# Two attentions of a four-layer fp32 kernel: transposed output, tokens as weights, and tanh read from PSUM

## The chip, the cores and the metric

The kernel runs on one core of a Trainium2 chip. One launch computes a whole network of four layers. The metric is device time in microseconds (us). Before the change it is 10574.42 us, the median of 3 runs (10572.73 to 10580.19).

Engines are named as in the profile: PE is the matrix engine's matmul and PEld its weight load, DVE the vector engine, ACT the scalar engine, POOL GpSimd, SP the engine that issues transfers. Everything is fp32.

## The reference, cut to what matters

The input is 4 images of 56 x 56 tokens with 128 channels, so S = 3136 tokens an image. Layers 0 and 1 (a windowed attention and a selective scan) and the two feed-forward parts are not touched by the change. The two attentions that are:

```python
def _L2_attn_ref(x, W1, b1, w2, b2):             # x: layer norm of t
    f = jnp.einsum('bih,ha->bia', x, W1[:h])     # a: 16 hidden units
    g = jnp.einsum('bjh,ha->bja', x, W1[h:])
    t = jnp.tanh(f[:, :, None, :] + g[:, None, :, :] + b1)
    scores = jnp.einsum('bija,a->bij', t, w2[:, 0]) + b2[0]
    flag = jnp.tril(jnp.ones((n_seq, n_seq)), -1)     # key j before query i only
    e = jnp.exp(scores) * flag
    w = e / (jnp.sum(e, axis=-1, keepdims=True) + 1e-10)
    return jnp.einsum('bij,bjh->bih', w, x)

def _L3_attn_ref(x):                             # x: layer norm of t
    scores = jnp.einsum('bsd,btd->bst', x, x)
    return jnp.einsum('bst,btd->bsd', jax.nn.softmax(scores, axis=-1), x)

def _ln_t(v, eps=1e-5):                          # normal over channels: they sum to zero
    m = jnp.mean(v, axis=-1, keepdims=True)
    return (v - m) / jnp.sqrt(jnp.var(v, axis=-1, keepdims=True) + eps)
...
t = t + _L2_attn_ref(_ln_t(t), ...)
t = t + _L2_ffn_ref(_ln_t(t), ...)
t = t + _L3_attn_ref(_ln_t(t))
t = t + _L3_ffn_ref(_ln_t(t), ...)
```

Layer 2 takes a tanh for every pair of tokens and every one of 16 hidden units, for the lower triangle only. Layer 3 is a plain softmax attention of x with itself over the full square, and subtracts a constant (64) in place of the row maximum.

## The kernel before

The kernel is written in a tile framework that sets semaphores, gives out buffers of a pool (`bufs` of them for a tag) and orders each engine's instructions itself: an instruction that is ready early may be placed ahead of its place in the program. Tokens are cut into 28 tiles of TP = 112, and into 7 chunks of CH = 448 queries (TC = 4 tiles). `xT` is the normed image with channels on the partitions, `xa` the same with tokens on the partitions and a column of ones, so that the product with the weights `e` gives the sum of them in column 128.

```python
def normed(self, b, big, sm, psum, tag):
    xa = self.t(big, [TP, NT, C + 1], "xa")
    self.nc.gpsimd.memset(xa[:, :, C : C + 1], 1.0)
    self.layer_norm(b, sm, xa)
    xT = self.t(big, [P, S], "xT")
    for c in range(NCH):
        self.transposed_chunk(psum, tag, xa, c, xT[:, c * CH : (c + 1) * CH])   # 4 transposes, one copy on DVE or ACT in turn
    return xa, xT
```

Layer 2. One tanh instruction takes 8 keys x 16 hidden units on the 128 partitions and 448 queries in the free dimension; its bias is `g`, one value a partition. A key tile of 112 tokens needs NG = 14 of them. A matmul with 32 columns of weights (`place`) sums the hidden units and puts the 8 rows where they belong.

```python
for b in range(B):
    xa, xT = self.normed(b, big, sm, ps_m, "m")
    fT = self.t(big, [P, S], "fT")
    for c in range(NCH):                       # line 821: 7 matmuls and 7 copies an image
        ps = self.t(ps_m, [P, 512], "m")
        nc.tensor.matmul(ps[:, :CH], wf..., xT[:, c * CH : (c + 1) * CH], start=True, stop=True)
        nc.vector.tensor_copy(fT[:, c * CH : (c + 1) * CH], ps[:, :CH])
    ps = self.t(ps_m, [P, 512], "m")
    for j in range(JG): ...                    # line 828: 8 matmuls for g
    g = ...
    for c in range(NCH):
        self.additive_chunk(b, c, xa, fT, g, b2, place, later, sm, ps_s, ps_o)

def additive_chunk(self, b, c, xa, fT, g, b2, place, later, sm, ps_s, ps_o):
    po = [self.t(ps_o, [P, 512], f"o{s}") for s in range(TC)]      # four banks
    for J in range(TC * (c + 1)):              # key tiles up to the diagonal
        k = max(J - TC * c, 0)
        lo = k * TP
        ps = self.t(ps_s, [P, 512], "s")
        for q in range(TC):
            for blk in range(4):
                n = 4 * blk + q
                if n >= NG: continue
                th = self.t(sm, [P, CH], "th", bufs=8)
                at = NG * J + n
                nc.scalar.activation(          # line 852
                    th[:, lo:], fT[:, c * CH + lo : (c + 1) * CH], AF.Tanh, bias=g[:, at : at + 1])
                ...
                nc.tensor.matmul(              # line 857
                    ps[QW * blk : QW * blk + rows, lo:CH], place[:, off : off + rows], th[:, lo:], ...)
        e = self.t(sm, [TP, CH], "e", bufs=3)
        nc.scalar.activation(e[:, lo:], ps[:TP, lo:CH], AF.Exp, bias=b2)       # line 862
        if J >= TC * c:
            nc.gpsimd.tensor_mul(e[:, lo : lo + TP], e[:, lo : lo + TP], later)
        for s in range(k, TC):                 # line 866: e is the weight, 129 columns stream
            nc.tensor.matmul(
                po[s][:TP, : C + 1], e[:, s * TP : (s + 1) * TP], xa[:, J, :],
                start=(J == 0), stop=(J == TC * c + s))
    self.attended(b, c, po, 1e-10, sm)

def attended(self, b, c, po, eps, sm):
    for s in range(TC):
        den = self.t(sm, [TP, 1], "den", bufs=4)
        nc.vector.tensor_scalar(den, po[s][:TP, C : C + 1], eps, None, op0=ALU.add)
        nc.vector.reciprocal(den, den)
        x = self.X[b][:, TC * c + s, :]
        nc.vector.scalar_tensor_tensor(x, po[s][:TP, :C], den, x, op0=ALU.mult, op1=ALU.add)
```

Layer 3, the attention of one image:

```python
xa, xT = self.normed(b, big, sm, ps_s, "s")
for c in range(NCH):
    po = [self.t(ps_o, [P, 512], f"o{s}") for s in range(TC)]
    for t in range(NT):                        # 28 key tiles of 112
        ps = self.t(ps_s, [P, 512], "s")
        nc.tensor.matmul(                      # line 1050
            ps[:TP, :CH], xT[:, t * TP : (t + 1) * TP], xT[:, c * CH : (c + 1) * CH], start=True, stop=True)
        e = self.t(sm, [TP, CH], "e", bufs=3)
        nc.scalar.activation(e, ps[:TP, :CH], AF.Exp, bias=shift)              # line 1055
        for s in range(TC):                    # line 1057
            nc.tensor.matmul(
                po[s][:TP, : C + 1], e[:, s * TP : (s + 1) * TP], xa[:, t, :],
                start=(t == 0), stop=(t == NT - 1))
    self.attended(b, c, po, 0.0, sm)
```

Of the kernel before, what the change touches and what calls it, by code (L numbers as in the profile page):

```python
# [10 lines left out]
AF = mybir.ActivationFunctionType  # L11
# [45 lines left out]
def host_constants():  # L57
# [11 lines left out]
    p = np.arange(P)  # L69
    place = np.zeros((P, QW + QW - JG), np.float32)  # L70
# [4 lines left out]
    for q in range(QG):  # L75
        pick[:, q, :] = (p % HD // 8 == q)[:, None] & (p[None, :] // DS == p[:, None] % 8)
        back[p, q, 8 * q + p // DS] = 1.0
    return {
        "k_state": (p[None, :] % DS == np.arange(DS)[:, None]).astype(np.float32),
# [9 lines left out]
class Hybrid:  # L89
# [688 lines left out]

    def normed(self, b, big, sm, psum, tag):

        xa = self.t(big, [TP, NT, C + 1], "xa")
        self.nc.gpsimd.memset(xa[:, :, C : C + 1], 1.0)  # L782
        self.layer_norm(b, sm, xa)
        xT = self.t(big, [P, S], "xT")
        for c in range(NCH):
            self.transposed_chunk(psum, tag, xa, c, xT[:, c * CH : (c + 1) * CH])
        return xa, xT

    def layer2_attention(self):
        nc, a, tc = self.nc, self.a, self.tc  # L790
        with ExitStack() as ctx:
# [17 lines left out]
            later = self.load(wp, [TP, TP], "later", a["k_later"])  # L809

            big = ctx.enter_context(tc.tile_pool(name="l2_big", bufs=2))
            sm = ctx.enter_context(tc.tile_pool(name="l2_sm", bufs=2))
            ps_m = ctx.enter_context(tc.tile_pool(name="l2_m", bufs=2, space=PSUM))
            ps_s = ctx.enter_context(tc.tile_pool(name="l2_s", bufs=2, space=PSUM))
            ps_o = ctx.enter_context(tc.tile_pool(name="l2_o", bufs=1, space=PSUM))
            for b in range(B):
                xa, xT = self.normed(b, big, sm, ps_m, "m")
                fT = self.t(big, [P, S], "fT")
                for c in range(NCH):
                    ps = self.t(ps_m, [P, 512], "m")  # L820
                    nc.tensor.matmul(
                        ps[:, :CH], wf.rearrange("p j a -> p (j a)"), xT[:, c * CH : (c + 1) * CH],
                        start=True, stop=True,
                    )
                    nc.vector.tensor_copy(fT[:, c * CH : (c + 1) * CH], ps[:, :CH])
# [8 lines left out]
                for c in range(NCH):  # L834
                    self.additive_chunk(b, c, xa, fT, g, b2, place, later, sm, ps_s, ps_o)

    def additive_chunk(self, b, c, xa, fT, g, b2, place, later, sm, ps_s, ps_o):
        nc = self.nc
        po = [self.t(ps_o, [P, 512], f"o{s}") for s in range(TC)]
        for J in range(TC * (c + 1)):  # L840
            k = max(J - TC * c, 0)
            lo = k * TP
            ps = self.t(ps_s, [P, 512], "s")

            for q in range(TC):
                for blk in range(4):
                    n = 4 * blk + q
                    if n >= NG:
                        continue
                    th = self.t(sm, [P, CH], "th", bufs=8)  # L850
                    at = NG * J + n
                    nc.scalar.activation(  # L852
                        th[:, lo:], fT[:, c * CH + lo : (c + 1) * CH], AF.Tanh, bias=g[:, at : at + 1]
                    )
# [10 lines left out]
            for s in range(k, TC):  # L865
                nc.tensor.matmul(  # L866
                    po[s][:TP, : C + 1], e[:, s * TP : (s + 1) * TP], xa[:, J, :],
                    start=(J == 0), stop=(J == TC * c + s),
                )
        self.attended(b, c, po, 1e-10, sm)  # L870

    def attended(self, b, c, po, eps, sm):

        nc = self.nc
        for s in range(TC):
            den = self.t(sm, [TP, 1], "den", bufs=4)
            nc.vector.tensor_scalar(den, po[s][:TP, C : C + 1], eps, None, op0=ALU.add)  # L877
            nc.vector.reciprocal(den, den)
            x = self.X[b][:, TC * c + s, :]
            nc.vector.scalar_tensor_tensor(x, po[s][:TP, :C], den, x, op0=ALU.mult, op1=ALU.add)  # L880
# [147 lines left out]
    def layer3(self, attention=True, ffn=True):  # L1028
        nc, a, tc = self.nc, self.a, self.tc
        with ExitStack() as ctx:  # L1030
# [5 lines left out]
            shift = self.t(wp, [TP, 1], "shift")  # L1036
            nc.vector.memset(shift, SHIFT3)

            big = ctx.enter_context(tc.tile_pool(name="l3_big", bufs=2))
            sm = ctx.enter_context(tc.tile_pool(name="l3_sm", bufs=2))  # L1040
            ps_s = ctx.enter_context(tc.tile_pool(name="l3_s", bufs=4, space=PSUM))
            ps_o = ctx.enter_context(tc.tile_pool(name="l3_o", bufs=1, space=PSUM))
# [136 lines left out]
```

## Time and profile before

The profiled execution took 10590.0 us. The stages, with the busy time of the engines in each, from the profile's view by stretches of time:

| stage | from, to (us) | length | PE | ACT | DVE | granted PE clock |
|---|---|---|---|---|---|---|
| layer 0 | 0 to 1050 | 1050 | 860.93 | 255.03 | 452.68 | 0.82 |
| layer 1 | 1050 to 4371 | 3321 | 2972.43 | 1712.61 | 2982.67 | 0.89 |
| layer 2, attention, 4 images | 4371 to 8191 | 3820 | see below | see below | 127.78 | 1.00 |
| layer 2, feed-forward | 8191 to 8694 | 503 | 404.83 | 49.86 | 148.72 | 0.51 |
| layer 3, attention of image 0 | 8694 to 9045 | 351 | see below | see below | 20.18 | 0.99 |
| layer 3, feed-forward of image 0 | 9045 to 9170 | 125 | 92.57 | 8.70 | 103.25 | 0.80 |

The last two rows come again for images 1 to 3. The four attentions of layer 3, from the first matmul of line 1050 to the end of the last of line 1057, take 350.2, 348.9, 347.9 and 348.5 us.

How to read it: a row of instruction groups names line, engine, operation, the tile written and the tile read, their shapes, the count, busy time, the mean of one in ns, and the idle time of that engine just before, with what ended it. An fp32 matmul is two records in the trace, each with a weight load of its own: the 784 x 4 matmuls of line 1057 are 6272 records. A row of the timeline has start, length, engine, line, operation and how many like instructions were merged. The length of a merged row runs from the first start to the last end, and neighbours overlap.

### The profile page before, as it was taken

The page shows a single profiled execution, that of the slowest core. Times are in us where ns is not written, and L with a number is a line of the kernel's source. Part 1 is how long each engine was busy: PE and PEld are TensorE (multiplying, and loading weights), DVE is VectorE, ACT ScalarE, POOL GpSimd, SP SyncE. Part 2 cuts the span into 40 slices and gives each one's busy share as a digit, 9 for nine tenths or more (in the row PEclk, how much of TensorE's full clock was granted, in tenths as well). Part 3 has the DMA queues.
Part 4 walks back from the last instruction along what each step waited for, and adds up shares of the span by engine and source line. Part 5 has one row for each costly group of instructions (what it writes and reads, how often), then busy time and mean ns, then how long its engine had stood idle before and what let it go on. Part 6 is the DMA issues. An engine that isn't in the chain of part 4 may idle for free.

```text
span 10590.0 us, 117304 instructions
## 1 busy us (share of the span) xinstructions
PE 9694.1 (92%) x45951; PEld 4085.7 (39%) x45951; DVE 4189.2 (40%) x8326; ACT 6116.9 (58%) x10038; POOL 2520.1 (24%) x1478
## 2 busy tenths in 40 slices
PE   7888799999899999899999999999999799898998
PEld 3333233333333333333333333333332586565665
DVE  3444798999998989500000000000000310413223
ACT  2222455555555555599989989998998103232222
POOL 0000577777777777200000000000000000000000
PEclk8788888998999889899999999999999559999999
DMA  2000000000000000000000000000000120000000
GB/s 40 1 1 6 5 1 1 1 1 1 1 1 1 1 1 1 1 1 1 1 1 1 1 1 1 1 1 1 1 1 15 39 78 1 7 1 7 1 7 7
DMA packets 90718, 61.20 MB, mean 6 GB/s; under 512 B 20635, under 2 KB 81587, under 8 KB 89971
## 3 DMA queue, kind: packets, MB, share of 16 engines
q1 hardware_dynamic: 90165, 53.70, 1.9%
q8 instruction: 362, 5.93, 0.2%
q14 instruction: 191, 1.56, 0.1%
HBM read 46.61 MB, written 7.07 MB: 5 GB/s over the span
## 4 chain that ended last, share of the span: by engine, by line
PE 74%; DVE 11%; ACT 9%; issue 4%; POOL 1%; SPq 0%; DMA 0%; ACTq 0%; DVEq 0%; POOLq 0%
PE s L857 27%; PE o L1057 7%; PE s L1050 6%; DVE hs L573 5%; PE a L551 5%; PE o L866 4%; PE m L680 4%; ACT e L862 2%; PE y L583 2%; PE d L407 2%; PE o L407 2%; PE s L390 2%; PE s L1127 1%; PE u L558 1%; DVE dBu L568 1%
## 5 line engine op out<-in xcount | busy, mean ns | idle before, releaser
L852 ACT ACTIVATE th<-fT,g 128x448 f32<-128x448 f32 (+3 forms) x6272 | 3328.9, 622 | 17.5 <-DVE g L833 17.5
L857 PE MATMUL s<-th,place 128*32 128x448 f32 (+4 forms) x12544 | 3182.7, 516 | 7.0 <-ACT th L852 7.0
L577 POOL TENSOR_TENSOR hs<-hs,bc 128x896 f32<-128x896 f32 x896 | 1857.8, 2082 | 701.0 <-DVE hs L573 588.2
L877 DVE TENSOR_SCALAR den<-o 112x1 f32<-112x1 f32 x224 | 31.8, 152 | 4961.7 <-PE o L866 3642.8
L573 DVE TENSOR_TENSOR_SCAN hs<-a,dBu 128x448 f32<-128x448 f32 x1792 | 1847.7, 1072 | 161.7 <-POOL hs L577 86.1
L857 PEld LDWEIGHTS s<-th,place 128*32 128x32 f32 (+1 forms) x12544 | 787.0, 106 | 2131.0 <-ACT th L852 2031.5
L561 ACT ACTIVATE a<-a 128x896 f32<-128x896 f32 x896 | 808.5, 902 | 953.2 <-PE u L558 442.3
L551 PE MATMUL a<-delta,A_pick 32*128 32x448 f32 x3584 | 1079.8, 638 | 96.7 <-DVE hs L573 92.4
L558 PE MATMUL u<-du,pick 32*128 32x448 f32 x3584 | 1034.7, 657 | 32.1 <-DVE dBu L568 27.8
L568 DVE TENSOR_TENSOR dBu<-u,bc 128x448 f32<-128x448 f32 x1792 | 1016.9, 609 | 46.5 <-PE u L558 41.3
L1055 ACT ACTIVATE e<-s,shift 112x448 f32<-112x448 f32 x784 | 496.3, 634 | 887.7 <-PE s L1050 840.3
L864 POOL TENSOR_TENSOR e<-e,later 112x112 f32<-112x112 f32 x112 | 47.2, 422 | 3814.4 <-ACT e L862 3814.4
L1057 PEld LDWEIGHTS o<-xa,e 112*112 112x112 f32 x6272 | 711.1, 176 | 297.5 <-ACT e L1055 295.6
L1057 PE MATMUL o<-xa,e 112*112 112x129 f32 x6272 | 789.3, 279 | 13.5 <-ACT e L1055 0.9
L1050 PE MATMUL s<-xT 128*112 128x448 f32 x1568 | 655.9, 540 | 0.0
L551 PEld LDWEIGHTS a<-delta,A_pick 32*128 32x128 f32 x3584 | 338.4, 202 | 707.5 <-issue 326.4
L866 PE MATMUL o<-xa,e 112*112 112x129 f32 x3248 | 492.3, 288 | 105.5 <-ACT e L862 98.1
L866 PEld LDWEIGHTS o<-xa,e 112*112 112x112 f32 x3248 | 384.5, 176 | 446.3 <-ACT e L862 402.2
L395 ACT ACTIVATE e<-s 112x896 f32<-112x896 f32 (+1 forms) x272 | 206.4, 801 | 601.8 <-PE s L390 434.7
L583 PE MATMUL y<-hs,sum 128*32 128x448 f32 x3584 | 495.7, 628 | 3.6 <-POOL hs L577 3.6
L782 POOL MEMSET xa<- 112x28 f32 x12 | 1.6, 148 | 1822.0 <-DVE X L880 1280.2
L558 PEld LDWEIGHTS u<-du,pick 32*128 32x128 f32 x3584 | 300.2, 204 | 302.9 <-DVE dBu L568 300.1
(225 smaller groups left out, 8436.3 us busy)
## 6 DMA issues: line engine op xcount, KB each, us to landing
w<-in_L_ffn_weight SPq DMA_DIRECT2D x16, 1024.0 KB
w<-in_L_ffn_weight SPq DMA_DIRECT2D x64, 256.0 KB
X<-in_x SPq DMA_DIRECT2D x8, 784.0 KB
out<-X SPq DMA_DIRECT2D x8, 784.0 KB
e_edge<-dtab SPq DMA_DIRECT2D x42, 49.0 KB
cw<-in_L_conv_conv_w SPq DMA_DIRECT2D x1, 1024.0 KB
e_inner<-dtab SPq DMA_DIRECT2D x14, 49.0 KB
dtab<-tab SPq DMA_DIRECT2D x1, 637.0 KB
```

What stands on the lines that cost most here:

```text
L551: nc.tensor.matmul(A[p][:, k], w["A"][own, l, f, q, :], pre[j]["delta"][own, f], start=True, stop=True,)
L558: nc.tensor.matmul(U[p][:, k], w["pick"][own, q, :], pre[j]["du"][own, f], start=True, stop=True)
L561: nc.scalar.activation(A[p], A[p], AF.Exp)
L568: nc.vector.tensor_mul(V[p][:, k], u[:, k], pre[p // PAIRS]["bc"][:, 0])
L573: nc.vector.tensor_tensor_scan(HS[p][:, k], A[p][:, k], V[p][:, k], 0.0, op0=ALU.mult, op1=ALU.add)
L577: nc.gpsimd.tensor_mul(HS[p], HS[p], bc[:, 1:2].to_broadcast([P, 2, CH]))
L583: nc.tensor.matmul(py[j, f][r * HD : (r + 1) * HD, :], w["sum"][:, q, :], HS[p + r // 2][:, r % 2], start=False, stop=(q == QG - 1),)
L852: nc.scalar.activation(th[:, lo:], fT[:, c * CH + lo : (c + 1) * CH], AF.Tanh, bias=g[:, at : at + 1])
L857: nc.tensor.matmul(ps[QW * blk : QW * blk + rows, lo:CH], place[:, off : off + rows], th[:, lo:], start=(q == 0), stop=(n + 1 == NG or q = ...
L866: nc.tensor.matmul(po[s][:TP, : C + 1], e[:, s * TP : (s + 1) * TP], xa[:, J, :], start=(J == 0), stop=(J == TC * c + s),)
L1050: nc.tensor.matmul(ps[:TP, :CH], xT[:, t * TP : (t + 1) * TP], xT[:, c * CH : (c + 1) * CH], start=True, stop=True,)
L1057: nc.tensor.matmul(po[s][:TP, : C + 1], e[:, s * TP : (s + 1) * TP], xa[:, t, :], start=(t == 0), stop=(t == NT - 1),)
```

## The change

The product of weights and values is turned around in both attentions. Before, the weights `e` were the array's stationary operand, in four pieces of 112 queries, and 129 columns of values streamed through. Afterwards the values (`xa[:, J, :]`, tokens on the partitions) are stationary and all 448 queries stream in one matmul; the result `po` has channels on the partitions and lies in one bank. No column is left over for the ones, so they take the place of channel 127, and `attended` turns the result back with a constant matrix `back`: an identity whose column 127 is -1 in every other row (the normed channels sum to zero) and whose column 128 picks the sum of the weights.

Besides, in layer 2 the first term `f` is no longer copied to SBUF: it is computed a chunk at a time into its own pool of two PSUM banks, and tanh reads it there. Its buffers `th` go from 8 to 12. In layer 3 the keys are cut into 25 tiles (24 of 128 and one of 64) in place of 28 of 112, for which the values are transposed again from `xT` into `xk`, and the program puts the product of a tile two tiles after its scores.

```diff
+    back_out = np.eye(P, P + 1, dtype=np.float32)
+    back_out[:, P - 1] = -1.0
+    back_out[P - 1, P - 1] = 0.0
+    back_out[P - 1, P] = 1.0
...
-        xa = self.t(big, [TP, NT, C + 1], "xa")
-        self.nc.gpsimd.memset(xa[:, :, C : C + 1], 1.0)
+        xa = self.t(big, [TP, NT, C], "xa")
... layer 2
+            ps_f = ctx.enter_context(tc.tile_pool(name="l2_f", bufs=2, space=PSUM))
-            ps_o = ctx.enter_context(tc.tile_pool(name="l2_o", bufs=1, space=PSUM))
+            ps_o = ctx.enter_context(tc.tile_pool(name="l2_o", bufs=2, space=PSUM))
             for b in range(B):
                 xa, xT = self.normed(b, big, sm, ps_m, "m")
-                fT = self.t(big, [P, S], "fT")
-                for c in range(NCH):
-                    ... (7 matmuls into ps_m, 7 copies to fT)
+                nc.gpsimd.memset(xa[:, :, C - 1 : C], 1.0)
...
                 for c in range(NCH):
-                    self.additive_chunk(b, c, xa, fT, g, b2, place, later, sm, ps_s, ps_o)
+                    f = self.t(ps_f, [P, 512], "f")[:, :CH]
+                    nc.tensor.matmul(f, wf..., xT[:, c * CH : (c + 1) * CH], start=True, stop=True)
+                    po = self.additive_chunk(c, xa, f, g, b2, place, later, sm, ps_s, ps_o)
+                    self.attended(b, c, po, 1e-10, back, sm, ps_m, "m")
... additive_chunk
-        po = [self.t(ps_o, [P, 512], f"o{s}") for s in range(TC)]
+        po = self.t(ps_o, [P, 512], "o")[:, :CH]
-                    th = self.t(sm, [P, CH], "th", bufs=8)
+                    th = self.t(sm, [P, CH], "th", bufs=12)
-                    nc.scalar.activation(
-                        th[:, lo:], fT[:, c * CH + lo : (c + 1) * CH], AF.Tanh, bias=g[:, at : at + 1]
-                    )
+                    nc.scalar.activation(th[:, lo:], f[:, lo:], AF.Tanh, bias=g[:, at : at + 1])
-            for s in range(k, TC):
-                nc.tensor.matmul(po[s][:TP, : C + 1], e[:, s * TP : (s + 1) * TP], xa[:, J, :], ...)
+            nc.tensor.matmul(po[:, lo:], xa[:, J, :], e[:, lo:], start=(J == 0), stop=(J == last))
... attended
+        oT = self.t(sm, [P, CH], "oT")
+        nc.vector.tensor_copy(oT, po)
+        for s in range(0, TC, 2):
+            ps = self.t(psum, [P, 512], tag)[:TP, : 2 * (C + 1)].rearrange("p (k c) -> p k c", k=2)
+            for k in range(2):
+                nc.tensor.matmul(
+                    ps[:, k, :], oT[:, (s + k) * TP : (s + k + 1) * TP], back, start=True, stop=True)
+            den = ... (as before, two tiles at a time; reads ps)
... layer 3
+                    tiles = [(k, min(P, S - k)) for k in range(0, S, P)]
+                    xk = self.t(big, [P, len(tiles), C], "xk", bufs=1)
+                    for t0 in range(0, len(tiles), 4):
+                        ps = self.t(ps_s, [P, 4, C], "s")
+                        for i, (k, n) in enumerate(tiles[t0 : t0 + 4]):
+                            nc.tensor.transpose(ps[:n, i, :], xT[:, k : k + n], self.ident)
+                        self.copy(xk[...], ps[...])
+                    nc.gpsimd.memset(xk[:, :, C - 1 : C], 1.0)
                     for c in range(NCH):
-                        po = [self.t(ps_o, [P, 512], f"o{s}") for s in range(TC)]
+                        po = self.t(ps_o, [P, 512], "o")[:, :CH]
... (scores and exp as before, on tiles[t], through ps_q of 3 banks; e has 4 buffers)
+                        for t in range(len(tiles) + 2):
+                            if t < len(tiles):
+                                weights(t)
+                            if t >= 2:
+                                n = tiles[t - 2][1]
+                                nc.tensor.matmul(
+                                    po, xk[:n, t - 2, :], es.pop(t - 2)[:n],
+                                    start=(t == 2), stop=(t == len(tiles) + 1))
-                        self.attended(b, c, po, 0.0, sm)
+                        self.attended(b, c, po, 0.0, back, sm, ps_s, "s")
```

## The prediction

> **What bounds the two stages now.** The change touches two stages only: the attention of layer 2 (3820 us) and four attentions of layer 3 (350.2 + 348.9 + 347.9 + 348.5 = 1395.5 us). I read the view by stretches of time first, for which engine is full where. Columns after the length are busy time (and count) of PE, PEld, DVE, ACT and POOL, then the granted clock.
>
> ```profile
> 4371.00:8191.00 3820.00, 3704.90 (x15962) 1195.70 (x15962) 127.78 (x554) 3560.26 (x6736) 47.53 (x114) 1.00 0.00 1
> 8694.00:9045.00 351.00, 347.65 (x1964) 235.26 (x1963) 20.18 (x131) 126.66 (x198) 0.07 (x1) 0.99 0.00 1
> ```
>
> PE is 97% busy in layer 2 and 99% in layer 3, but the busy time of pipelined matmuls overlaps waiting, so it decides nothing. ACT is 93% busy in layer 2 and 36% in layer 3. The waits between 4400 and 5300 us say who holds whom in layer 2:
>
> ```profile
> PEld s L857 <- ACT th L852: 494.6, 1204, 0.5
> ACT e L862 <- PE s L857: 48.2, 100, 0.6
> ```
>
> The weight load waits for tanh 494.6 us out of 900, while ACT never waits for a tanh buffer, only 48.2 us for the scores before an exp. So **layer 2 is bound by ACT**: one tanh, and PE follows. (The chain of waits puts 27% of the span on line 857 of PE. That is because it steps back along PE where PE and ACT touch; the wait above is the better witness.) The timeline of ACT gives the rates:
>
> ```profile
> 6030.62 7.92 ACT L852 ACTIVATE th<-fT,g 128x448 f32<-128x448 f32 x14
> 6039.07 0.63 ACT L862 ACTIVATE e<-s,b 112x448 f32<-112x448 f32 x1 [0.53 <-PE s L857]
> 6039.60 5.69 ACT L852 ACTIVATE th<-fT,g 128x448 f32<-128x448 f32 x10
> ...
> 9172.37 1.68 ACT L1055 ACTIVATE e<-s,shift 112x448 f32<-112x448 f32 x3
> ```
>
> 14 tanh in 7.92 us, the last 0.657 long (median of line 852): (7.92 - 0.657) / 13 = **0.559 us from one tanh to the next**. The exp of line 862 reads PSUM, is 0.634 long (median), and the next tanh starts 0.53 after it. The last row is the one place where exps of the same 448 elements follow each other without a gap, PSUM to SBUF with a bias by partition, the tanh's form after the change: three in 1.68 us. Their own starts in the trace are 0.532 and then 0.517 apart, in each of images 1, 2 and 3; the first of a train starts from rest. So a steady train from PSUM has **0.517**.
>
> Layer 3 has another pattern. The timeline of PE:
>
> ```profile
> 8746.09 1.67 PE L1050 MATMUL s<-xT 128*112 128x448 f32 x4
> 8747.79 2.02 PE L1057 MATMUL o<-xa,e 112*112 112x129 f32 x16
> 8749.64 1.67 PE L1050 MATMUL s<-xT 128*112 128x448 f32 x4
> 8751.35 2.02 PE L1057 MATMUL o<-xa,e 112*112 112x129 f32 x16
> ```
>
> Two key tiles take 8749.64 - 8746.09 = 3.55 us: 4 score records (2 tiles), then 16 records of the product. Single starts: a score record follows the last after 0.375 us, a product record after 0.110; from the last score record to the first product it is 0.571 and from there to the second 0.201. So 4 x 0.375 + 16 x 0.110 = 3.26 is streaming and 0.29 is a wait for the exp of the first tile (its weights are e, so even the load can't start). **Layer 3 is bound by PE**, at 1.777 us a tile: 784 tiles x 1.777 = 1393 of the 1395.5 us.
>
> [...] Here a load of 112 columns is recorded at 177 ns and records follow at 110, so loads are hidden where their data is there.
>
> **Layer 2, part by part.**
> - *tanh from PSUM.* On the path. A key tile of full width has 14 tanh; 13 intervals save 0.559 - 0.517 = 0.042 and the last one 0.023 to 0.03 (0.657 against 0.634 or 0.627): 13 x 0.042 + 0.027 = 0.573 us. The saving is in the fixed part, so the narrow tiles at the diagonal (0.465, 0.372, 0.278 now) save the same. 448 tiles (4 images x 4 x (1 + ... + 7)) x 0.573 = **257 us**. The wait before exp (203 us in all) stays: it is two records of the last matmul, which the change leaves.
> - *Product turned around.* 3248 records x 0.110 = 357 us of PE become 896 records, 364 tiles at full width and 84 at 3/4, 1/2, 1/4: 364 x 0.75 + 28 x (0.56 + 0.375 + 0.19) = 305 us. Off the path: **0**.
> - *f by the chunk.* At the head of an image, 14 records of line 821 with 7 copies, some 6.6 us between 4351.6 and 4358.7, stand before the g of line 828, and ACT is idle there (20 us from 5311.4 to 5331.5 between images). They leave that place: 4 x 6 = about **24 us**. A later chunk's f needs only xT and a free bank of two, so I expect it to be placed early, in PE's pauses.
> - *attended.* A copy of po (DVE, 0.62 as the 128 x 448 copies of line 825) and 8 records of 129 columns, 0.9 us of PE, beside ACT's tanh; 12 th buffers cover 6 us. But its tiles come from the pool `ps_m` where the next image's transposes wait for ACT copies. I put down 3.5 us an image for such meetings: **-14 us**.
>
> Sum for layer 2: 257 + 24 - 14 = **267 us**.
>
> **Layer 3, part by part.**
> - *Fewer tiles.* 25 of up to 128 rows in place of 28: 700 in place of 784. 84 x 1.50 = 126 us.
> - *Product turned around.* Two records of 0.375 in place of eight of 0.110: 0.13 us x 784 = 102 us.
> - *The wait.* e is now the moving operand and two tiles old; its weights xk are there early. 0.147 us x 784 = 115 us.
>  Together 1393 - 700 x 4 x 0.375 = 1393 - 1050 = **343 us**.
> - *attended.* 8 records of 129 columns on PE, which is the bound here: 0.9 us if the loads hide, and po has one bank, so the next product waits for the copy; the next scores can fill that. 1.3 us x 28 chunks = **-36 us**.
> - *xk.* 25 transposes and 7 copies an image, and one memset over all of xk that holds the first product: about 4 us x 4 = **-16 us**.
>
> Sum for layer 3: 343 - 36 - 16 = **291 us**. ACT has an exp every 0.52 of 1.5 us and isn't near its limit. Total: 10574 - 267 - 291 = **10016 us**.
>
> **Rivals.**
> - *A wait takes the place of f's copy.* If f's matmul stays at its place in program order, each chunk begins with exp (0.35), mask (0.42), product and f (0.9) before the first tanh: some 2.4 us x 28 = 67 us less. [...] Against it: the trace shows transposes of the next image placed in the middle of the present one.
> - *Tanh gains less.* The 0.517 rests on a few pairs; at 0.532 it would be 6272 x 0.027 = 169 us, 90 less.
> - *PE's boundary in layer 3.* If the scores of the next chunk don't fill the copy of po, or every change of weights costs a load of about 0.1 us, 28 x 1 or 700 x 0.1: 30 to 70 us less.
> - *The boundary between images goes.* If g of the next image also moves ahead, the other 14 us of ACT's pause go too: 3 x 14 = 42 us more.
>
> **Range and chances.** The sure part is layer 3's count of records (343) and tanh's fixed cost (169 to 257). With the first three rivals together the time is about 10016 + 67 + 60 = 10145; with the last, 9975, and 9940 with boundaries at nothing. I take 9935 to 10135. 2% is 211 us, and each stage alone would pass it, so faster is near certain.
>
> **What would show it.** Tanh reading f with 0.517 from start to start, a key tile in 8.4 us in place of 8.95, the layer 2 stage near 3550 us; f's matmul amid an earlier chunk; in layer 3 records 0.375 apart with no wait for exp and an attention of 276 us an image. Wrong it would be if tanh kept 0.53 or more, if ACT waited for f at chunk heads, or if PE paused at weight changes.

## The result: 10102.92 us, and where the time went

The changed kernel takes **10102.92 us** (median of 3 runs, 10101.16 to 10105.18) against 10574.42: ratio 0.9553, 95% interval [0.9531, 0.9575], 471.5 us less. That lies in the predicted range, 87 us above the predicted 10016. In the later comparisons each kernel was timed beside the kernel before, whose median was then 10564 to 10577 us; layers 0 and 1, whose code is the same in all of them, reach their last exp on ACT between 4284 and 4316 us in the profiled runs. A difference of some 30 us or less between two kernels is therefore read from the lengths of the stages, not from the totals.

By stages, from the two traces:

| part | before | after | saved | predicted |
|---|---|---|---|---|
| four images of layer 2, first tanh to last exp | 3756.1 | 3564.6 | 192 | 257 |
| the three stretches between them, to the next tanh | 61.5 | 73.6 | -12 | see next row |
| last exp of layer 1 to the first tanh | 57.2 | 51.1 | 6 | 24 - 14 for f and attended, in all places |
| four attentions of layer 3 | 1395.5 | 1099.4 | 296 | 343 - 36 = 307 |
| the stretches after each of them | 499.8 | 515.9 | -16 | -16 (xk) |

Together 466 us against 558 predicted. First the view by stretches of time (busy time and count of PE, PEld, DVE, ACT and POOL, then the granted clock), the attention of layer 2 and that of one image in layer 3:

```profile
4339.00:7988.00 3649.00, 3469.21 (x13853) 981.97 (x13851) 126.78 (x593) 3358.76 (x6742) 47.20 (x115) 1.00 0.00 1
8894.00:9168.00 274.00, 273.52 (x748) 134.75 (x746) 20.89 (x104) 113.53 (x179) 0.14 (x1) 1.00 0.00 0
```

The stage of layer 2 is 3649 us in place of 3820; the prediction named 3550. An image of layer 3 is 274 with 748 PE records in place of 351 with 1964; the prediction named 276. The waits in layer 2, 4400 to 5200 us (total, count, longest):

```profile
PEld s L865 <- ACT th L862: 468.7, 1177, 0.7
...
ACT e L870 <- PE s L865: 48.8, 95, 0.6
```

The same two as before: PE's weight load waits for tanh, ACT only for the scores before an exp. ACT is still the bound. The timeline of ACT (start, length of the merged row, what, count, idle before):

```profile
5649.74 0.63 ACT L870 ACTIVATE e<-s,b 112x448 f32<-112x448 f32 x1 [0.50 <-PE s L865]
5650.27 7.45 ACT L862 ACTIVATE th<-f,g 128x448 f32<-128x448 f32 x14
5658.23 0.64 ACT L870 ACTIVATE e<-s,b 112x448 f32<-112x448 f32 x1 [0.50 <-PE s L865]
```

A key tile takes 5658.23 - 5649.74 = 8.49 us (predicted 8.4, before 8.95). The starts of the 14 tanh are 0.516 to 0.517 us apart, as predicted. But their durations aren't alike: single records grow from 0.627 for the first to 0.736 for the last, 0.0084 more each time. So their **ends** are (7.45 - 0.627) / 13 = 0.525 us apart. Before, all 14 lasted 0.655 to 0.658 and starts and ends both had 0.559.

And PE in layer 3, at the end of one chunk of image 1:

```profile
9004.90 0.92 PE L1092 MATMUL o<-e,xk 128*128 128x448 f32 x2
9005.65 0.92 PE L1080 MATMUL q<-xT 128*128 128x448 f32 x2
9006.40 0.92 PE L1092 MATMUL o<-e,xk 128*128 128x448 f32 x2
9007.24 0.97 PE L1080 MATMUL q<-xT 128*64 128x448 f32 x2
9008.14 2.72 PE L1092 MATMUL o<-e,xk 128*128 128x448 f32 x6
9010.79 1.77 PE L1080 MATMUL q<-xT 128*128 128x448 f32 x4
9012.39 1.04 PE L884 MATMUL s<-back,oT 128*112 128x129 f32 x8
```

Each row of two records is one matmul. They start 0.75 us apart, scores and product in turn, and nobody waits for an exp. `attended` (line 884) costs PE its eight records of 0.11 and no pause: two scores of the next chunk stand before it and cover the copy of `po`. Only around the 64-wide last tile is there something more: 9006.40 to 9007.24 is 0.84, not 0.75.

### The profile page after: what moved, and what is told of

It reads as the page before. It is cut to its first block, busy times and chain, and to the rows that moved or that the text cites. A ratio compares the mean times of both kernels' runs of the same rounds, so it can differ in the third digit from the quotient of the medians.

```text
span 10099.4 us, 103168 instructions
## 1 busy us (share of the span) xinstructions
PE 9160.8 (91%) x39107; PEld 3482.4 (34%) x39107; DVE 4185.1 (41%) x8144; ACT 5868.1 (58%) x9972; POOL 2520.2 (25%) x1474
## 4 chain that ended last, share of the span: by engine, by line
PE 74%; DVE 12%; ACT 9%; issue 4%; POOL 1%; SPq 0%; DMA 0%; ACTq 0%; DVEq 0%; POOLq 0%
PE s L865 27%; DVE hs L580 5%; PE o L1092 5%; PE q L1080 5%; PE a L558 5%; PE o L873 4%; PE m L687 4%; ACT e L870 3%; PE y L590 2%; PE d L414 2%; PE o L414 2%; PE s L397 2%; PE u L565 2%; PE s L1162 1%; DVE dBu L575 1%
## 5 line engine op out<-in xcount | busy, mean ns | idle before, releaser
L862 ACT ACTIVATE th<-f,g 128x448 f32<-128x448 f32 (+3 forms) x6272 | 3119.8, 646 | 22.0 <-DVE g L836 22.0
L865 PE MATMUL s<-th,place 128*32 128x448 f32 (+4 forms) x12544 | 2966.9, 516 | 8.9 <-ACT th L862 8.3
L880 DVE COPY oT<-o 128x448 f32<-128x448 f32 x56 | 35.0, 625 | 4207.4 <-PE o L873 3234.0
L575 DVE TENSOR_TENSOR dBu<-u,bc 128x448 f32<-128x448 f32 x1792 | 1015.3, 607 | 47.5 <-PE u L565 43.1
L1085 ACT ACTIVATE e<-q,shift 128x448 f32<-128x448 f32 (+1 forms) x700 | 443.2, 634 | 638.3 <-PE q L1080 635.3
L1092 PE MATMUL o<-e,xk 128*128 128x448 f32 (+1 forms) x1400 | 639.8, 543 | 0.4
L1080 PE MATMUL q<-xT 128*128 128x448 f32 (+1 forms) x1400 | 640.1, 542 | 0.0
L873 PE MATMUL o<-e,xa 112*128 112x448 f32 (+3 forms) x896 | 425.9, 557 | 164.1 <-POOL e L872 92.5
L870 ACT ACTIVATE e<-s,b 112x448 f32<-112x448 f32 x448 | 268.6, 600 | 218.5 <-PE s L865 218.4
L406 DVE TENSOR_TENSOR e<-e,e_inner 112x560 f32<-112x560 f32 (+5 forms) x416 | 238.3, 612 | 350.4 <-ACT e L402 350.3
```

Source lines behind the costliest of these rows:

```text
L575: nc.vector.tensor_mul(V[p][:, k], u[:, k], pre[p // PAIRS]["bc"][:, 0])
L862: nc.scalar.activation(th[:, lo:], f[:, lo:], AF.Tanh, bias=g[:, at : at + 1])
L865: nc.tensor.matmul(ps[QW * blk : QW * blk + rows, lo:CH], place[:, off : off + rows], th[:, lo:], start=(q == 0), stop=(n + 1 == NG or q = ...
L873: nc.tensor.matmul(po[:, lo:], xa[:, J, :], e[:, lo:], start=(J == 0), stop=(J == last))
L1080: nc.tensor.matmul(ps[:n, :CH], xT[:, k : k + n], xT[:, c * CH : (c + 1) * CH], start=True, stop=True,)
L1092: nc.tensor.matmul(po, xk[:n, t - 2, :], es.pop(t - 2)[:n], start=(t == 2), stop=(t == len(tiles) + 1),)
```

## The experiments

**1. The source of tanh alone: f copied to SBUF again.** Everything else as after the change.

```diff
+ fs = self.t(sm, [P, CH], "fs")
+ nc.vector.tensor_copy(fs, f)
- po = self.additive_chunk(c, xa, f, ...)
+ po = self.additive_chunk(c, xa, fs, ...)
```

> The changed kernel, but f is copied from PSUM to SBUF by DVE and tanh reads it there: the one step that reads from PSUM undone. Theory (0.525 against 0.559 a tanh, with the wait before exp 0.034 shorter again): 448 x 0.43 = 193 us more, about 10295 us. As predicted beforehand (0.517): 257 us more, 10360 us.

Measured: 10295.39 us, ratio 0.9741 [0.9727, 0.9756], 192 us more than the changed kernel (195 by the four images: 3759.5 us). ACT's timeline:

```profile
5701.28 0.63 ACT L872 ACTIVATE e<-s,b 112x448 f32<-112x448 f32 x1 [0.47 <-PE s L867]
5701.82 7.92 ACT L864 ACTIVATE th<-fs,g 128x448 f32<-128x448 f32 x14
5710.20 0.63 ACT L872 ACTIVATE e<-s,b 112x448 f32<-112x448 f32 x1 [0.47 <-PE s L867]
```

The row of 14 tanh is 7.92 again, a tile 8.92, and the wait before exp 0.47 in place of 0.50. So reading PSUM is worth 192 us, not 257, and a part of the faster train goes into that wait: 204.3 us in all here, 218.5 in the changed kernel. The rest of the change in layer 2 (turned product, 12 buffers, `attended`) is still in this run, and its images take 3759.5 us against 3756.1 before the change: within an image it costs or gives next to nothing.

**2. Does a tanh take 0.517 or 0.525? The exp taken out of the train's end.** In the changed kernel each train of 14 ends in a wait for PE, so it never becomes steady. Here the exp of a key tile comes after the first 4 tanh of the next one, and ACT has no reason to stop.

```diff
+ count += 1
+ if count == 4 and late:
+     late.pop()()             # exp, mask and product of the tile before
... (late is a list of one image; attended follows the last product of a chunk)
- e = ...; nc.scalar.activation(e[:, lo:], ps[:TP, lo:CH], AF.Exp, bias=b2)
- ... (mask, product)
+ late.append(finish)          # the same lines, as a function
+ if c == NCH - 1: late.pop()()        # the last tile of an image
```

> The changed kernel, but the exp of a key tile in layer 2 (with mask and product) is placed after the first four tanh of the next key tile, so ACT has no wait for the scores and its trains of tanh are not broken. Theory (a tanh from PSUM leaves ACT every 0.525 us; the recorded starts, 0.517 apart, only run ahead of that): a full key tile takes 15 x 0.525 = 7.88 us in place of 8.49, so 448 x 0.61 = 273 us less, about 9830 us, and the starts themselves stretch to 0.525 once the lead can't grow. Rival (0.517 holds, the growing ends are how the trace shows them): 15 x 0.517 = 7.76 us, about 9775 us. Rival (PE is the hidden limit behind tanh): little is won, 10000 us or more.

Measured: 9819.8 us, ratio 0.9295 [0.9278, 0.9312]. An image of layer 2 takes 822.9 us in place of 890.5; by its stage, from layer 1's last exp on, that is 270 us, by the totals 283.

```profile
5867.54 1.59 ACT L876 ACTIVATE e<-s,b 112x448 f32<-112x448 f32 x1
5868.07 8.40 ACT L863 ACTIVATE th<-f,g 128x448 f32<-128x448 f32 x14
5875.41 1.59 ACT L876 ACTIVATE e<-s,b 112x448 f32<-112x448 f32 x1
```

No idle time stands in the rows (the length of the row of 14 spans the exp between them), and a tile of 14 tanh and one exp takes 5875.41 - 5867.54 = 7.87 us: 7.87 / 15 = **0.5245 us an instruction**. At 0.517 it would be 7.76. Starts are still 0.516 apart, but only until the records are 1.6 to 1.7 us long (1.583 to 1.694, median 1.638, between 5849 and 5990 us): then one start in each tile, that of the exp, comes 0.624 after the one before it, and what the lead had grown is given back. Here starts run ahead of what the ends sustain by up to about a microsecond (1.694 against 0.627 for a record that follows a stop, 1.07); the ends keep the rate. The run shows a second thing too: the stop at the end of each train, which the prediction left in place, was worth more than the change of source: 67.6 us an image are 112 tiles x 0.60. Of this 0.49 is the idle time before exp (218.5 us in 448 tiles), which is gone. The other 0.11 is not idle time: an exp that comes after a stop takes its full 0.634 us from start to end, while in a train that goes on each instruction adds only 0.5245.

**3. Do matmuls slow ACT down? 4 of 14 `place` matmuls.** The other ten tanh are computed and read by nobody; scores and output differ from the reference's. The numbers are those of a single execution.

```diff
+ if q == (1 if blk == 3 else TC - 1):       # the last of each 32 rows only
      nc.tensor.matmul(ps[...], place[...], th[:, lo:], start=True, stop=True)
```

> The changed kernel, but in layer 2 only 4 of the 14 place matmuls of a key tile are done (the last of each column group), so 10 of 14 tanh tiles are never read by PE and most of PE's reads and PSUM writes beside tanh are gone. The output is not the reference's. Theory (0.5245 us from the end of one tanh to the end of the next is ACT's own rate from PSUM to SBUF): ends stay 0.5245 apart, starts 0.516, an image takes about 891 us as before. Rival (the 8 ns above 0.516 come from PE using SBUF and PSUM at the same time): ends go to 0.516 to 0.518, some 12 us less an image.

Measured: 10325.41 us. The train of 14 is as long as in the changed kernel, 7.45 us:

```profile
5605.22 7.45 ACT L862 ACTIVATE th<-f,g 128x448 f32<-128x448 f32 x14
```

Tanh's starts stay 0.517 apart and its ends 0.525: PE's reading isn't what holds ACT. But the kernel became slower. Its stage in the view by stretches, and ACT's wait:

```profile
4327.00:8219.00 3892.00, 2522.87 (x4894) 572.20 (x4892) 127.41 (x597) 3358.92 (x6743) 47.25 (x114) 0.59 0.00 0
```

```profile
ACT e L871 <- PE s L866: 460.6, 447, 1.4
```

The clock granted to PE is 0.59 in place of 1.00, with 4894 records in place of 13853. A tile's first `place` matmul, two records, takes 1.67 us (at 5609.05), where in the changed kernel the second record of a tile's last one starts 0.400 after the first and lasts 0.539, 0.94 together (medians); the wait before exp is 460.6 us in place of 218.5. Over the whole execution the granted clock is 0.76 against 0.91. The 0.41 that this stage lost, by its share of the span (3892 of 10323.6 us), make 0.155: by this estimate the stage alone accounts for the difference. What takes the clock down was not shown. ACT's busy time is the same within 0.2 us (3358.92 against 3358.76).

**4. Does the target of the write set the rate? Tanh into PSUM.** 11 of 14 tanh write to PSUM and are read by nobody; their matmuls read a constant tile (output not the reference's). First with one bank for them:

```diff
... (ps_d, of one bank, taken from po; the matmuls of the discarded tanh read a constant tile)
- th = self.t(sm, [P, CH], "th", bufs=12)
+ th = self.t(sm, [P, CH], "th", bufs=12) if q == TC - 1 else self.t(self.ps_d, [P, 512], "d")[:, :CH]
```

> The changed kernel, but the first 11 tanh of a key tile write a PSUM bank that nobody reads, and their place matmuls read a constant tile in its place; the last 3 write SBUF and are read. The output is not the reference's. Theory (reading from PSUM allows a tanh every 0.516 us, and writing to SBUF one every 0.5245): with PSUM as the target the ends are no more than 0.516 apart, and durations don't grow over the first 11. Rival (the 0.5245 is set by the instruction or its bias, whatever the target): ends stay 0.5245 apart.

Measured: 10694.7 us, inconclusive: ten tanh in a row take 6.37 us and eight 5.09, so each started (6.37 - 5.09) / 2 = 0.64 us after the one before it, which wrote to the same bank, and with two banks, below, the starts are 0.516 apart. The one thing it gives is that a record into PSUM is shorter: 5.09 - 7 x 0.64 = 0.61 us, and 0.60 for the first of a train below, against 0.627 into SBUF. Then with two banks (one of them taken from `ps_m`; the eleven matmuls stay and read the constant tile, though the expectation below has them left out):

> In layer 2 the first 11 of a key tile's 14 tanh write to PSUM, into two banks in turn, and are read by nobody; their matmuls are left out (output not the reference's). What is wanted is the distance between ends of tanh. Theory: the 0.5245 us between ends belongs to the write to SBUF; into PSUM ends and starts are both 0.516 us or less apart and durations don't grow along a train. Rival: 0.5245 us is ACT's rate for 448 elements read from PSUM whatever it writes to; then ends are 0.5245 apart here too and durations grow by 8 ns a tanh. If one tanh waits for the bank of the one two before it, neither can be read.

Measured: 10256.6 us in one execution, and ACT's timeline, `d` being the discarded ones:

```profile
5727.99 5.32 ACT L869 ACTIVATE d<-f,g 128x448 f32<-128x448 f32 x10
5733.15 1.76 ACT L869 ACTIVATE th<-f,g 128x448 f32<-128x448 f32 x3
```

Ten into PSUM take 5.32 and the first four of them 2.17: (5.32 - 2.17) / 6 = 0.525 from end to end. The starts are (5733.15 - 5727.99) / 10 = 0.516 apart, so durations grow here too, from 2.17 - 3 x 0.525 = 0.60 for the first to 5.32 - 9 x 0.516 = 0.68 for the tenth. The rival holds: the rate is the same 0.525 for both targets. (In this kernel the granted clock was 0.85 and some waits were longer, so its total says nothing.) What inside ACT makes 0.5245 of 0.517 stays open.

**5. The pauses between images: a bank of its own for `attended`.**

```diff
- ps_o = ctx.enter_context(tc.tile_pool(name="l2_o", bufs=2, space=PSUM))
+ ps_o = ctx.enter_context(tc.tile_pool(name="l2_o", bufs=1, space=PSUM))
+ ps_a = ctx.enter_context(tc.tile_pool(name="l2_a", bufs=1, space=PSUM))
- self.attended(b, c, po, 1e-10, back, sm, ps_m, "m")
+ self.attended(b, c, po, 1e-10, back, sm, ps_a, "a")
```

> The changed kernel, but attended in layer 2 takes its PSUM tile from a pool of its own (one bank, taken from po, which has one in place of two), not from the pool that the transposes of the next image use. Theory (sharing that pool keeps the next image's transposes behind the last attended of this one): transposes are placed ahead again, ACT's pause between images goes from 24.6, 23.3 and 22.9 us to about 14, some 28 us less: about 10075 us. Rival (the pause is set by the matmuls of g and the norm): unchanged, 10100 us.

Measured: 10060.31 us, ratio 0.9521 [0.9507, 0.9535]. Images of 889.9 us (890.5 in the changed kernel), stretches of 16.4, 17.2 and 16.4 between them in place of 26.0, 24.6 and 23.0. By its stage that is 27 us; the totals say 43. ACT's waits in the first pause, in the changed kernel:

```profile
ACT xT L128 <- PE m L149: 8.7, 4, 4.4
ACT L862 <- DVE ln_q L141: 7.4, 1, 7.4
ACT ln_r L136 <- DVE ln_ve L134: 4.7, 1, 4.7
```

and with the bank of its own:

```profile
ACT L863 <- DVE g L837: 12.6, 1, 12.6
```

Layer norm and transposes of the next image stand in the pause of the changed kernel. With `attended` out of `ps_m` most of them are placed ahead again, as they were before the change, and only g is waited for. What stays of the rival is that wait, 12.6 us.

**6. Layer 3's change taken back.** Layer 2 as after the change, layer 3's attention as before it.

```diff
- tiles = [(k, min(P, S - k)) for k in range(0, S, P)] ... (xk, lag of two tiles, one po, attended with back)
+ ... (the attention of layer 3 of the kernel before: 28 tiles, four po of 129 columns)
```

> The changed kernel with the layer 3 attention of the kernel before in full (28 tiles of 112, e as weights, no xk). Theory (layer 3 gave 296 us in its matmuls and takes 16 back between images for xk): 280 us more, about 10383 us, attentions of 348 us in place of 274. Rival (part of the gain seen in layer 3 comes from elsewhere): 250 us more or less.

Measured: 10362.62 us, ratio 0.9805 [0.979, 0.982], 260 us more than the changed kernel. The four attentions take 1394.0 us (before 1395.5), the stretches after them 498.6: 277 us more than in the changed kernel, which the theory had at 280; the 260 of the totals hold the noise of the other layers. So layer 3 is as slow as before when its own code is put back, whatever layer 2 does, and the two halves of the change add up.

**7. Layer 3 without the lag.** The product of a tile right after its scores in the program.

```diff
- for t in range(len(tiles) + 2): ... product of tile t - 2
+ for t in range(len(tiles)):     ... product of tile t
```

> The changed kernel, but in layer 3 the product of a key tile follows its own scores and exp in the program, not two tiles later. Theory (the wait for the exp went because e is the moving operand and is two tiles old): without the lag the order on each engine is left to the framework, which put two scores ahead of two products before; some wait comes back, 0.1 to 0.2 us a tile in 700 tiles: 70 to 140 us more, 10175 to 10245 us. Rival (the framework finds the same order by itself): 10103 us.

Measured: 10173.31 us, ratio 0.9625 [0.9611, 0.964]; an attention of 295.8 us in place of 273.8. PE:

```profile
9050.85 1.67 PE L1080 MATMUL q<-xT 128*128 128x448 f32 x4
9052.55 1.77 PE L1092 MATMUL o<-e,xk 128*128 128x448 f32 x4
9054.16 1.67 PE L1080 MATMUL q<-xT 128*128 128x448 f32 x4
```

The framework again puts two tiles of scores before two products, as in the kernel before, and the wait for the exp is back: a score record to a product record is 0.571, as before the change, where the changed kernel has 0.376. Two tiles take 3.31 us in place of 3.00. The lag is worth 88 us over the four attentions (by the totals the kernel is 70 us slower).

**8. Layer 3 in 28 tiles of 112, no `xk`.**

```diff
- tiles = [(k, min(P, S - k)) for k in range(0, S, P)]
+ tiles = [(k, TP) for k in range(0, S, TP)]
- xk = ... (25 transposes, 7 copies)
+ xk = xa
```

> The changed kernel, but layer 3 keeps 28 key tiles of 112, so that xa serves as it is (its channel 127 set to one) and xk with its transposes is gone. Theory (a record costs its 448 columns whatever its rows): 84 more tiles of 1.5 us, 126 us more, and some 16 us less for xk: about 10213 us, attentions of 305 us. Rival (112 rows stream faster or slower than 128): it differs from this by the change in the 0.375 us of a record.

Measured: 10184.4 us, ratio 0.9637 [0.9621, 0.9653]. The four attentions take 1208.0 us, 43.1 a chunk: 28 x 1.5 + 1.1. In this kernel too the records are 0.375 to 0.380 us apart, with 112 rows of weights in place of 128 in the product and 112 columns in the scores. So the turned product and the gone wait are worth 1395.5 - 1208.0 = 187 us with attended paid, and the tiles of 128 another 109. The stretches after the attentions are 500.4 us, as before the change: the 16 us more of the changed kernel are `xk`.

**9. The last tile padded to 128.** Padded keys have zero values and a zero in the column of ones; the result is unchanged.

```diff
- tiles = [(k, min(P, S - k)) for k in range(0, S, P)]
+ tiles = [(k, P) for k in range(0, S, P)]
+ xp = self.t(big, [P, P], "xp", bufs=1)          # last 64 keys, then zeros
+ nc.gpsimd.memset(xp, 0.0)
+ nc.vector.tensor_copy(xp[:, :real], xT[:, S - real : S])
... (scores and xk of the last tile read xp; the column of ones is set for the real keys alone)
```

> The last key tile of layer 3 is padded with zero channels-by-token columns to 128 keys, so that all 25 tiles have the same size of weights (its padded keys have zero values and a zero in the column of ones; the result is unchanged). Theory: the records around the 64-wide tile are 0.43 to 0.48 us apart in place of 0.375 only because the weight load isn't hidden when the tile's size changes; 0.74 us x 28 chunks = about 20 us less than the changed kernel, near 10083 us, an attention of 269 us in place of 273.8, all score and product records 0.375 apart. Rival: those gaps come from the end of a chunk (the last exp, the product that lags two tiles, the result copied out), then the time stays near 10103 us and the gaps stay where they are.

Measured: 10071.79 us, ratio 0.9535 [0.9522, 0.9548]. By the totals that is 31 us less than the changed kernel and by the ratios 19, with intervals that overlap; the stage decides. The four attentions take 1078.4 us in place of 1099.4, the last three 268.91 each. The same place in a chunk:

```profile
8913.81 0.92 PE L1098 MATMUL o<-e,xk 128*128 128x448 f32 x2
8914.57 0.91 PE L1086 MATMUL q<-xT,xp 128*128 128x448 f32 x2
8915.32 2.42 PE L1098 MATMUL o<-e,xk 128*128 128x448 f32 x6
8917.57 1.67 PE L1086 MATMUL q<-xT 128*128 128x448 f32 x4
```

The six product records take 2.42 in place of 2.72, and every record of this stretch follows the last after 0.375 or 0.376. The tile with half the weight columns takes PE no less time than a full one (0.90 us for its two score records, from 9007.24 to 9008.14 in the changed kernel, against 0.75), and with its borders 0.74 us a chunk more, 21 us in all. What stands in those gaps can be read from the weight loads of the changed kernel:

```profile
9006.40 0.19 PEld L1092 LDWEIGHTS o<-e,xk 128*128 128x128 f32 x1 [0.19 <-issue]
9007.24 0.19 PEld L1080 LDWEIGHTS q<-xT 128*64 128x64 f32 x2 [0.65 <-issue]
9012.02 0.18 PEld L884 LDWEIGHTS s<-back,oT 128*112 128x112 f32 x1 [0.19 <-issue]
```

The load at 9006.40 belongs to the record at 9006.77: it starts a whole record ahead. The one of the 64-wide tile starts at 9007.24 together with its own record, 0.469 after the record before. But it isn't any change of size that does this: the load of `attended`'s 112 columns (9012.02) is a record ahead again, and its first record follows after 0.376. Why the loads of the narrow tile are not early stays open.

**10. All of it together.** The exp late, over chunks and images too; the bank of its own; the statistics of the layer norm of all four images ahead of the first; the copies of the transposes on DVE alone; the padded tile.

```diff
+ got = [self.layer_norm_stats(b, sm, B) for b in range(B)]     # ahead of the loop over images
- xa, xT = self.normed(b, big, sm, ps_m, "m")
+ xa, xT = self.normed(b, big, sm, ps_m, "m", got[b])
- if c == NCH - 1: late.pop()()
+ if c == NCH - 1 and b == B - 1: late.pop()()
... (copies of the transposes on DVE; with the edits of 2, 5 and 9)
```

> The changed kernel with everything that the runs point to: layer 2's exp of a key tile after the first 4 tanh of the next one, across chunks and images too; attended with a PSUM bank of its own; the layer-norm statistics of all 4 images computed ahead of the first one; the copies of the transposes in layer 2 on DVE alone; layer 3's last key tile padded to 128. Theory, by the single runs: -283 (exp late), -43 (own bank), up to -45 (three boundaries of 15 us, if the next image's g is ready when the last tanh ends), -20 (pad): 10103 - 391 = 9712 us, a layer 2 attention of about 822 us an image with no pause between images. Rival: the parts take the same idle time twice (own bank and the exp carried over both fill the boundary), then near 9765 us.

Measured: 9799.18 us, ratio 0.9276 [0.9263, 0.9289]: neither 9712 nor 9765. There is no pause between images any more, and from the first tanh to the last exp it is 3330.6 us. But four images of 822.9 are 3291.6. At the head of image 1, ACT:

```profile
5217.83 7.41 ACT L884 ACTIVATE th<-f,g 128x448 f32<-128x448 f32 x14
5227.24 0.63 ACT L897 ACTIVATE e<-s,b 112x448 f32<-112x448 f32 x1 [2.00 <-PE s L887]
...
5242.28 0.45 ACT L897 ACTIVATE e<-s,b 112x224 f32<-112x224 f32 x1 [3.25 <-PE s L887]
...
5250.37 0.35 ACT L897 ACTIVATE e<-s,b 112x112 f32<-112x112 f32 x1 [2.89 <-PE s L887]
...
5263.55 0.63 ACT L897 ACTIVATE e<-s,b 112x448 f32<-112x448 f32 x1 [5.48 <-PE s L887]
```

14.2 us of waits for the scores here, as many at the head of image 2, 9.0 at that of image 0: 3291.6 + 37.4 = 3329 us, all but 2 of the 3330.6. In PE's rows of this stretch the transposes and the g of the image after stand between the score matmuls, each of the eight pieces of g as long as this one:

```profile
5242.04 1.65 PE L853 MATMUL m<-xT,wg 128*128 128x392 f32 x2
```

The last image, which no image follows, has no wait at its head. The work moved out of the pause to the place where the key tiles are narrow and few, and there PE was late. The statistics of images 1 to 3 cost 22.1 us of waits ahead of the first tanh.

**11. Three parts alone: exp late, own bank, padded tile.**

> Three parts alone: layer 2's exp of a key tile after the first 4 tanh of the next tile, attended with a PSUM bank of its own, layer 3's last key tile padded to 128. The layer norm stays at the head of its image, as in the changed kernel. Theory: in the kernel with everything, the statistics of all four images ahead of the first cost about 24 us that the pauses had cost before, and the next image's transposes and g, once they no longer stand in a pause, held the scores up at the head of images 1 and 2 (14 us of waits before exp each); so nothing came of its hidden pauses. Without these two moves the single runs should add: -283 (exp late), -43 (own bank), -20 (pad), near 9757 us, with images of 823 us and pauses of 15 us. Rival: own bank lets the same transposes into the head of the image and the exp that trails there pays for it; then it is no better than the kernel with everything, near 9800 us.

```diff
... (the edits of 2, 5 and 9, and nothing else)
```

Measured: 9797.2 us (9778.4 to 9811.86), ratio 0.926 [0.9243, 0.9277]. Images of 822.9 us, stretches of 16.4, 17.2 and 16.4 between them (15.1 and 1.28 for a load of ACT's table of functions in the first), and 1079.8 us for the attentions of layer 3: each part does here what it did alone. The total is the rival's, 9800, but its mechanism isn't there: ACT waits for scores for 0.5 us between 4300 and 7800 us. The total is 40 us above the expected one because that was added up from totals. By the stages the parts are 270 (exp late), 27 (bank) and 20 (padded tile), and 10103 - 317 = 9786 us, 11 from the measured median. By stages this is the best kernel of all that ran, 11 us ahead of run 10 in layer 2; by the totals the two aren't told apart.

## Why the prediction was right, and where it was not

**Which engine bounds which stage** was right, and with it that the kernel gets clearly faster: ACT still holds PE in layer 2 (468.7 against 48.8 us in the waits), and PE streams in layer 3, without a gap but for the 64-wide tile. The terms that missed did not cancel: layer 2 gave 65 and 16 us less than predicted, layer 3 11 less.

**"A steady train from PSUM has 0.517": the step that failed.** The rate was taken from the starts of trains of three exps. Run 2 shows 0.5245 an instruction in a train that never stops, and run 4 the same between ends into PSUM. A train of 14 tanh went from 7.914 to 7.448 us (mean of the full tiles), and the narrow ones became shorter by as much (6.521 to 6.054 with 336 elements, 5.213 to 4.747 with 224, means of 28), so what is saved doesn't depend on the width, as the prediction assumed. 0.467 x 448 = 209 us, less the 15 by which the wait before exp grew (203.4 to 218.5 us): 194, against 192 measured by the trace and in run 1, and 257 predicted. The row in the prediction held the right number: three exps in 1.68 us with the first 0.634 long are (1.68 - 0.634) / 2 = 0.523; single ends in the trace are 0.524 and 0.525 apart. The starts of the same three, 0.532 and 0.517 apart, are what the prediction used; run 2 shows starts up to a microsecond ahead of what the ends sustain. That 0.517 is a steady rate was the author's estimate, and the ends decide.

**"The wait before exp stays"** was nearly right, 15 us off. In both kernels the first record of the last matmul starts 0.053 us after the last tanh's end and the second 0.400 later (medians of the full tiles); but from there to the exp it is 0.052 in place of 0.018, and 0.019 in run 1, where tanh reads SBUF. So the 0.034 a tile goes with the source of tanh and lies behind PE's last start; what takes it stays open.

**f by the chunk, +24, and attended, -14:** in place of +10 the two cost 6. The prediction saw that attended shares `ps_m` with the next image's transposes, but expected the price inside the chunks. There it cost nothing. It took away the placing ahead of those transposes, and the pauses grew by 12 us; run 5 shows the cause by taking 24 us off them. With that price gone, the three pauses are 11 us shorter than before the change and the way to the first tanh 4 us: that is what leaving out f's copies gave, about 16 us of the 24.

**The rival "ACT waits for f at chunk heads"** fell. In the whole execution tanh waits 22 us, all for g at the heads of images:

```profile
L862 ACT ACTIVATE th<-f,g 128x448 f32<-128x448 f32 (+3 forms) x6272 | 3119.8, 646 | 22.0 <-DVE g L836 22.0
```

**Turned product in layer 2, 0 us:** right. Among ACT's waits in the stage there is none that the product ends: only the scores before an exp (218.4 us), and what the head of an image needs. Run 1 agrees, with the turned product in it and images as long as before.

**Layer 3, 343 - 36 - 16:** 296 - 16. Run 8 splits the 343: product and wait 102 + 115 - 36 = 181 predicted, 187 measured; fewer tiles 126 predicted, 109 measured. The 17 us missing there are the 64-wide tile (run 9: 21 us), which the count of 0.375 a record did not foresee; attended cost 0.88 a chunk, 25 us, not 36. `xk` cost 16 as predicted. Run 7 gives the wait by itself as 88 us over 700 tiles, 0.126 a tile against 0.147 in the prediction. The weight loads that the prediction took for hidden are hidden, 0.376 from record to record, but for those of the 64-wide tile and of the one after it, up to 0.48: of the rival "every change of weights costs a load" that corner came true. Its 0.1 us was the author's estimate; those records show 0.05 to 0.10 more. That a record takes as long with 128 rows as with 112, on which the 126 us for fewer tiles rest, was an estimate too, and run 8 shows it: 0.375 to 0.380 with 112, 0.376 with 128.

**The range.** Its upper end is too low for its own rivals: 10016 + 67 + 60 takes in the first and the third and leaves out the 90 us of the second, tanh gaining less, with which it is 10233. The kernel came to lie inside because the second came true in part (65 us) and the other two hardly.

## What to carry to other kernels

Read the rate of ACT from the ends of a train, (length of the merged row - first record) / (count - 1), and look whether durations grow; here the starts ran ahead, 0.517 apart where the ends were 0.525. An engine that is the bound should not stand waiting for the result of its own last output: moving one exp four instructions later gave 270 us, about as much as the whole change in layer 3. A small new user of a shared PSUM pool cost here where the pool's other user was working ahead (12 us in the three pauses), and hidden work has to be hidden where the engine it runs on has room: moved to the head of an image it came back as 37.4 us of waits.

## What the hardware showed that was not expected

In these runs ACT gets through 448 elements a partition every 0.5245 us when it reads PSUM and writes SBUF (0.525 when it writes PSUM), and every 0.559 from SBUF to SBUF, while, from PSUM, the starts of its records go 0.516 apart until they lead by about a microsecond (1.07 us). Taking 10 of 14 matmuls away from PE made a kernel bound by ACT slower, 10325.41 us against 10102.92: the granted clock of the stage was 0.59 in place of 1.00 and the wait for the last matmul of a tile 460.6 us in place of 218.5. On PE a 64-wide tile between 128-wide ones streams no faster than they do (0.90 us for two records against 0.75), and the records at its borders are 0.43 to 0.48 us apart in place of 0.375; the step from 128 columns to 112 costs nothing (0.376).
